# Laying out anew the pieces of a sorted second layer between the steps of a pair product

## The chip, the cores and the metric

The program runs on one core of one Trainium2 chip. The metric is the device time of one execution in microseconds (us); the median of the runs shown of the kernel before is 933.59 us (three runs, 932.44 to 934.21). Five engines work side by side, each through its own queue of instructions: PE multiplies matrices (its weight loads are listed apart as PEld), DVE does vector work, ACT does activations, POOL issues the indirect transfers here, and SP issues most of the others.

## The reference

Two images of 256 channels and 64 x 64 points (N = 4096 points) go through two layers. The first one is a 3 x 3 convolution to 64 channels, a normalisation and a PReLU; the similarity of all points, a sparse softmax over each row, and a weighted sum back onto the image. The change is in the second layer alone:

```python
g_x = jnp.einsum('oc,bcn->bno', g_w, xf) + g_b
a = jnp.einsum('c,bcn->bn', w_t, theta)
bsc = jnp.einsum('c,bcn->bn', w_p, phi)
f = jax.nn.relu(a[:, :, None] + bsc[:, None, :] + wf_b[0])
y = jnp.matmul(f / N, g_x)
...
z = W_y + xf
```

For each point n the layer sums g over the points m with a(n) + b(m) above zero, each with that sum as its weight. Written out, y(n) is a(n) times a sum of g(m) plus a sum of b(m) g(m), over the points whose b is above -a(n). If the points are sorted by b, both sums are prefix sums, and one row of a table of prefix sums is all that a point needs.

## The kernel before

The program does the second layer in two ways, one for each image, and lets them run beside each other.

**Image 1: pairs** (`by_pairs`, L662). After `attend(1)` (first layer, L442: 16 groups of four matmuls, and one DVE addition `x<-av,x` at L458 for each of eight column blocks) it forms `ga1` (`project`, L460: matmuls at L465 and a DVE addition at L472), spreads the row a over all partitions (`spread`, L476), and then runs the pair product: four quarters q of 1024 columns, 32 steps m each. A step makes f = relu(a + b) into one of four buffers (ACT at L676; in the last quarter every second one by DVE at L678) and multiplies it with g on PE (L680). After each quarter `finish` (L486) is called for two halves: ACT scales the sum (L690), PE multiplies with `wz` (L491), ACT writes `w` (L493, a tile with two buffers, tag "wb"), DVE adds it to `x` (L494) and SP stores the output (L495).

**Image 0: ranks** (`by_rank`, L497). It has no loop of its own: it hands pieces to the object `Beside`, which keeps them with a planned time. Each `beside.step(dt)` in the loops of image 1 moves a planned clock on and emits into the program the pieces that have fallen due: 3.6 a step in `attend`, 1.5 in the projection, 1.75 in the pair product. What is left over comes at the end, by `beside.rest()`. The pieces, in their order:

- `start`: spreads the row b into `bb` (S4) and takes `junk` (S5).
- `rank(t)`, 32 times: DVE counts for 128 points how many lie above them (L525, L528, L531, two small operations at L535 and L536), and POOL scatters those rows of g and b to their rank in the DRAM table `sg` (L537).
- `sorted_in`: reads the sorted rows back as two half tables `tab` (L548; S4 and S6, where S6 is the slot of `ga0`), and spreads the row a into `ab` (S5, after `junk`), by a PE transpose (L479), an ACT copy and two transfers.
- `products(0)`, `products(1)`: b times g (L562, L563). `sums`: 31 additions down the table, a row of 257 numbers each (L572).
- `before`: one PE product for the sums of the partitions before (`po`, L576), two DVE additions of it to the tables (L579) and two transfers to the DRAM table `tb` (L582).
- `segments`: two DVE operations make `oh` (L590, L591; S3) out of `ab`. `places(i)`, four times: 8 PE products `pk` (L599) and four DVE operations give the row of the table for 1024 points.
- `fetch(t)`, 32 times: POOL gathers 128 rows of `tb` into `r` (L614; S3, after `oh`; 16 places for 32 fetches). `taken(i)`, eight times: DVE at L625, PE transposes at L628, ACT at L630, and `finish`.

The tags S0 to S6 are slots of one buffer each: a tile waits until the tile before it in its slot is no longer read. The order of the program is not the order on the engines. When the program is built, a scheduling pass orders the instructions of each engine and adds the waits[...]. In the trace the small fill of `cnt` (L512, in `start`) runs 1.18 us after the span begins, though it stands in the program behind the whole first layer.

Of the kernel before, what the change touches and what calls it, by code (L numbers as in the profile page):

```python
# [8 lines left out]
F32 = mybir.dt.float32  # L9
# [10 lines left out]
P = 128  # L20
HW = 64
N = HW * HW
CB = 512
NCB = N // CB
NT = N // P
# [7 lines left out]
UN = 2 * CB  # L33
# [4 lines left out]
CS = 2 * CI + 1  # L38
TW = N // P
TH = TW // 2  # L40
# [45 lines left out]
def sparse_path(ctx: ExitStack, tc, a, out, rows_i):  # L86
# [7 lines left out]
    room = ctx.enter_context(tc.tile_pool(name="room", bufs=1))  # L94
# [388 lines left out]
        nc.sync.dma_start(out=rd.rearrange("o (t p) -> (o t) p", p=P), in_=row[0:nt])  # L483
        nc.sync.dma_start(out=dst[:, ds(t0 * P, nt * P)], in_=rd.to_broadcast((P, nt * P)))

    def finish(b, yT, cols):  # L486

        ov = out[b].rearrange("(k p) n -> p k n", p=P)
        for ct in range(CT):
            pz = ps_av.tile([P, CB], F32, name=f"pz_{b}_{ct}_{cols.start}", tag="av")  # L490
            nc.tensor.matmul(pz, lhsT=wz_sb[:, ts(ct, P)], rhs=yT, start=True, stop=True)  # L491
            w = work.tile([P, CB], F32, name=f"w_{b}_{ct}_{cols.start}", tag="wb")
            nc.scalar.activation(w, pz, AF.Identity, bias=b1[:, ct : ct + 1], scale=s1[:, ct : ct + 1])  # L493
            nc.vector.tensor_add(xs[b][:, ct, cols], w, xs[b][:, ct, cols])  # L494
            nc.sync.dma_start(out=ov[:, ct, cols], in_=xs[b][:, ct, cols])  # L495

    def by_rank(b, ga, beside):  # L497

# [4 lines left out]
        d = {}  # L503
# [40 lines left out]
        def sorted_in():  # L544
            sv = d["sg"].rearrange("(p t) c -> p t c", p=P)
            d["tab"] = [room.tile([P, TH, CS], F32, name=f"tab_{b}_{h}", tag=f"S{4 + 2 * h}") for h in range(2)]
            for h in range(2):
                nc.sync.dma_start(out=d["tab"][h][:, :, 0 : CI + 1], in_=sv[:, ts(h, TH)])  # L548
            nxt = small.tile([P, 1], F32, name=f"nxt_{b}", tag="nxt")
            nc.vector.memset(nxt, -3.0e38)  # L550
            nc.sync.dma_start(out=nxt[0 : P - 1], in_=sv[1:P, 0, CI : CI + 1])
            d["nxt"] = nxt
            d["ab"] = room.tile([P, N], F32, name=f"ab_{b}", tag="S5")
            spread(b, ga, CI + 1, d["ab"], 0, NT)

        def products(h):
            tab = d["tab"][h]
            if h == 0:
                d["kr"] = small.tile([P, TW + 2], F32, name=f"kr_{b}", tag="kr")
                nc.vector.memset(d["kr"][:, TW : TW + 1], 1.0)  # L560
                nc.vector.tensor_scalar_mul(d["kr"][:, TW + 1 : TW + 2], lane, float(TW))
            nc.vector.tensor_copy(d["kr"][:, ts(h, TH)], tab[:, :, CI])  # L562
            nc.vector.tensor_mul(  # L563
                tab[:, :, CI + 1 : CS], tab[:, :, 0:CI], tab[:, :, CI : CI + 1].to_broadcast([P, TH, CI])
            )
# [4 lines left out]
        def sums(t0, t1):  # L570
            for t in range(max(1, t0), t1):
                nc.vector.tensor_add(at(t), at(t), at(t - 1))  # L572
# [10 lines left out]

        def segments():

            oh = room.tile([P, N], F32, name=f"oh_{b}", tag="S3")
            lim = small.tile([P, 2], F32, name=f"lims_{b}", tag="lims")
            nc.vector.tensor_scalar_mul(lim[:, 0:1], d["kr"][:, 0:1], -1.0)
            nc.vector.tensor_scalar_mul(lim[:, 1:2], d["nxt"], -1.0)
            nc.vector.tensor_scalar(oh, d["ab"], lim[:, 0:1], None, ALU.is_gt)  # L590
            nc.vector.scalar_tensor_tensor(oh, d["ab"], lim[:, 1:2], oh, ALU.is_le, ALU.mult)  # L591
            d["oh"] = oh
            d["k"] = small.tile([P, NT], U32, name=f"k_{b}", tag="k")
# [16 lines left out]

        def fetch(t):
            if t == 0:
                d["r"] = room.tile([P, TH, CS], F32, name=f"r_{b}", tag="S3")
            nc.gpsimd.indirect_dma_start(  # L614
                out=d["r"][:, t % TH],
                out_offset=None,
                in_=d["tb"],
                in_offset=bass.IndirectOffsetOnAxis(ap=d["k"][:, t : t + 1], axis=0),
            )
# [17 lines left out]

        beside.add(0.0, start)
        beside.add(1.0, lambda: nc.vector.tensor_copy(acol, ga[:, :, CI + 1]))
        for t in range(NT):  # L640
            beside.add(11.0 + 5.6 * t, lambda t=t: rank(t))
        t1 = 11.0 + 5.6 * NT
        beside.add(t1, sorted_in)
        t1 += 10.0
        beside.add(t1, lambda: products(0))
        beside.add(t1 + 2.5, lambda: products(1))
        beside.add(t1 + 5.0, lambda: sums(0, TH))
        beside.add(t1 + 12.0, lambda: sums(TH, TW))
        beside.add(t1 + 19.0, before)
        beside.add(t1 + 28.0, segments)  # L650
        for i in range(4):
            beside.add(t1 + 35.0 + 2.0 * i, lambda i=i: places(i))
        t1 += 43.0
        for t in range(TH):
            beside.add(t1, lambda t=t: fetch(t))
        for i in range(8):
            beside.add(t1 + 8.0 + 5.5 * i, lambda i=i: taken(i))
            if i < 4:
                for t in range(4):
                    beside.add(t1 + 9.0 + 5.5 * i, lambda t=TH + 4 * i + t: fetch(t))  # L660

    def by_pairs(b, ga, beside):  # L662

        ab = room.tile([P, N], F32, name=f"ab_{b}", tag="S1")
        for i in range(NU):
            for m in range(8 * i, 8 * i + 8, 3):
                project(b, ga, m, min(m + 3, 8 * i + 8))
                beside.step(1.5)
            spread(b, ga, CI + 1, ab, 8 * i, 8)
        f = room.tile([P, 4, UN], F32, name=f"f_{b}", tag="S2")  # L670
        for q in range(NU):
            py = ps_sim.tile([P, UN], F32, name=f"py_{b}_{q}", tag="sim")
            for m in range(NT):
                bm = ga[:, m, CI : CI + 1]
                if q < NU - 1 or m % 2 == 0:
                    nc.scalar.activation(f[:, m % 4, :], ab[:, ts(q, UN)], AF.Relu, bias=bm)  # L676
                else:
                    nc.vector.tensor_scalar(f[:, m % 4, :], ab[:, ts(q, UN)], bm, 0.0, ALU.add, ALU.max)  # L678
                for h in range(2):
                    nc.tensor.matmul(  # L680
                        py[:, ts(h, CB)],
                        lhsT=ga[:, m, 0:CI],
                        rhs=f[:, m % 4, ts(h, CB)],
                        start=(m == 0),
                        stop=(m == NT - 1),
                    )
                beside.step(1.75)
            for h in range(2):
                yT = work.tile([P, CB], F32, name=f"yT_{b}_{q}_{h}", tag="wa")
                nc.scalar.activation(yT, py[:, ts(h, CB)], AF.Identity, scale=1.0 / N)  # L690
                finish(b, yT, ds(q * UN + h * CB, CB))

    got = [{}, {}]
    beside = Beside()
# [423 lines left out]
```

## Time and profile before

| | |
|---|---|
| median of the runs shown | 933.59 us |
| profiled execution, its own time | 934.23 us |
| its span, first to last instruction | 931.9 us |
| PE busy | 823.0 us (88%) |
| DVE busy | 551.5 us (59%) |
| ACT busy | 374.4 us (40%) |
| POOL busy | 112.7 us (12%) |
| `attend(1)` to the last addition | from 511 to 925 us of the span |

The span is 2.33 us shorter than the profiled execution's own time, and that execution took 0.64 us more than the median. Times in the trace count from the start of the span. A matmul of 512 columns on PE is two entries of some 0.43 us each from start to start, so that a step m of the pair product (four entries) takes 1.72 us. "Idle before" is the time in which an engine stood still before an instruction, and the arrow names what ended it. The chain of waits goes back from the last instruction to what released it.

### The profile page before, as it was taken

The numbers are of one execution on the slowest core, as the hardware profiler recorded it, in microseconds if no ns is written. First come the engines' busy times: TensorE is split into PE (matmuls) and PEld (weight loads), VectorE is DVE, ScalarE is ACT, GpSimd is POOL, SyncE is SP. The second block draws the span as 40 slices with busy tenths as digits, with TensorE's granted clock in tenths as the row PEclk, the third lists the DMA queues.
The fourth block names the chain that finished last, engine by engine and source line by source line (L and its number), as shares of the span: only waits on it lengthen the run. The fifth ranks groups of instructions, "written<-read, shape, count | busy, mean of one in ns | idle before, by whom it ended". The sixth has DMA issues, their size and how long they took to land.

```text
span 931.9 us, 8237 instructions
## 1 busy us (share of the span) xinstructions
PE 823.0 (88%) x3080; PEld 383.5 (41%) x3080; DVE 551.5 (59%) x794; ACT 374.4 (40%) x487; POOL 112.7 (12%) x95
## 2 busy tenths in 40 slices
PE   7999999999978889999898997269961999997996
PEld 3664444443323334444355443144420444453442
DVE  0105777774278676778257799999984005635432
ACT  0003676630066756650026000036622667633542
POOL 0000000008100000007200011111120000026500
PEclk9997999999999999999899998599985999998998
DMA  9202000011120000001100200021003005225411
GB/s 364 70 12 57 1 1 0 1 46 40 23 58 0 1 1 0 1 1 47 27 1 1 94 10 15 12 80 34 15 14 94 0 1 181 114 86 152 146 69 72
DMA packets 27412, 45.21 MB, mean 49 GB/s; under 512 B 11777, under 2 KB 16738, under 8 KB 26594
## 3 DMA queue, kind: packets, MB, share of 16 engines
q1 hardware_dynamic: 23730, 36.36, 11.3%
q0 software_dynamic: 3200, 7.64, 3.1%
q8 instruction: 26, 0.43, 0.2%
q10 hardware_dynamic: 432, 0.59, 0.2%
q14 instruction: 24, 0.20, 0.1%
HBM read 25.60 MB, written 16.88 MB: 46 GB/s over the span
## 4 chain that ended last, share of the span: by engine, by line
PE 62%; DVE 27%; ACT 4%; DMA 3%; issue 2%; POOL 1%; ACTq 0%; DVEq 0%; SPq 0%; POOLq 0%
PE sv L271 20%; PE py L680 16%; PE cv L221 13%; DVE junk L528 8%; DVE junk L525 8%; PE av L449 6%; DVE mq L418 3%; PE pz L491 2%; DVE top L289 2%; PE rw L271 1%; ACT z L417 1%; ACT z L433 1%; DVE z L435 1%; DVE junk L531 1%; POOL r L614 1%
## 5 line engine op out<-in xcount | busy, mean ns | idle before, releaser
L680 PE MATMUL py<-f,ga 128*128 128x512 f32 x512 | 230.6, 603 | 33.3 <-ACT f L676 27.4
L271 PE MATMUL sv<-e 64*128 64x512 f32 x1024 | 236.8, 605 | 13.3 <-DVE top L289 6.9
L289 DVE MAX8 top<-sv 128x8 f32<-128x1024 f32 x128 | 157.3, 1231 | 59.7 <-PE sv L271 59.5
L285 ACT ACTIVATE sv<-sv,nthr 128x1024 f32<-128x1024 f32 x128 | 139.3, 1088 | 76.5 <-ACT sv L285 52.0
L676 ACT ACTIVATE f<-ab,ga 128x1024 f32<-128x1024 f32 x112 | 127.8, 1147 | 82.2 <-PE py L680 80.0
L680 PEld LDWEIGHTS py<-f,ga 128*128 128x128 f32 x512 | 97.3, 193 | 150.4 <-issue 116.6
L271 PEld LDWEIGHTS sv<-e 64*128 64x128 f32 x1024 | 99.8, 189 | 140.7 <-ACT sv L285 62.0
L221 PE MATMUL cv<-x,w_sb 128*64 128x504 f32 (+3 forms) x576 | 128.3, 602 | 6.6 <-DMA w_sb<-in_conv_w 5.9
L449 PE MATMUL av<-z,xb 128*128 128x512 f32 x256 | 117.5, 618 | 6.6 <-DVE rk L535 5.1
L221 PEld LDWEIGHTS cv<-x,w_sb 128*64 128x64 f32 x576 | 60.7, 141 | 70.4 <-issue 41.9
L449 PEld LDWEIGHTS av<-z,xb 128*128 128x128 f32 x256 | 50.0, 198 | 70.5 <-issue 60.0
L528 DVE TENSOR_SCALAR_CACHE_REDUCE junk<-bb,ga 128x4096 f32<-128x4096 f32 (+31 forms) x32 | 77.4, 2417 | 0.0
L525 DVE TENSOR_SCALAR_CACHE_REDUCE junk<-bb,ga 128x128 f32<-128x128 f32 (+30 forms) x31 | 72.8, 2347 | 0.0
L494 DVE TENSOR_TENSOR x<-w,x 128x512 f32<-128x512 f32 x32 | 21.9, 689 | 67.1 <-ACT w L493 67.1
L537 POOL DMA_INDIRECT sg<-ga,rank x32 | 31.0, 970 | 218.9 <-DVE junk L531 121.4
L465 PE MATMUL g<-gw_sb,x 128*128 128x130 f32 x256 | 34.6, 288 | 23.9 <-DVE rk L535 19.8
L360 POOL TENSOR_TENSOR x<-x,mask 128x4096 f32<-128x4096 f32 x4 | 31.8, 7979 | 187.9 <-DMA mask<-kd 187.9
L418 DVE MAX8 mq<-z 128x8 f32<-128x1024 f32 x32 | 38.8, 1223 | 24.0 <-ACT z L417 23.9
L230 ACT ACTIVATE y<-cv,b,s 128x512 f32<-128x512 f32 x8 | 6.2, 777 | 114.4 <-PE cv L221 99.2
L614 POOL DMA_INDIRECT r<-tb,k x32 | 32.5, 1017 | 149.3 <-DVE above L603 132.5
L417 ACT COPY z<-rw 128x1024 f32<-128x1024 f32 x32 | 31.7, 1012 | 43.8 <-PE rw L271 43.8
L232 DVE TENSOR_SCALAR t<-y,v 128x512 f32<-128x512 f32 x8 | 3.9, 485 | 75.5 <-ACT y L230 75.5
(152 smaller groups left out, 494.8 us busy)
## 6 DMA issues: line engine op xcount, KB each, us to landing
x<-in_x SPq DMA_DIRECT2D x16, 512.0 KB
out<-x SPq DMA_DIRECT2D x32, 256.0 KB
tb<-tab SPq DMA_DIRECT2D x2, 2056.0 KB
tab<-sg SPq DMA_DIRECT2D x2, 1032.0 KB
e<-e SPq DMA_DIRECT2D x16, 128.0 KB
et<-es SPq DMA_DIRECT2D x16, 128.0 KB
mask<-kd SPq DMA_DIRECT2D x2, 1024.0 KB
bb<-rd SPq DMA_DIRECT2D x1, 2048.0 KB
```

The lines of the kernel that those rows point to most:

```text
L221: nc.tensor.matmul(p3[ts(h, CR), r0 - R * j : r1 - R * j, c0:c1], lhsT=w_sb[:, kc, 3 * dy + dx], rhs=x4[:, kc, r0 + dy - 1 : r1 + dy - 1, ...
L271: nc.tensor.matmul(ps[:, ts(h, CB)], lhsT=lhs(h), rhs=e[ts(h, CR), q], start=True, stop=True)
L285: nc.scalar.activation(ps, ps, AF.Relu, bias=nthr[:, i : i + 1], accum_out=over[:, i // 2, q : q + 1])
L289: nc.vector.max(m8[:, i // 2, ts(q, 8)], ps)
L417: nc.scalar.copy(zs[k][:, ts(q, UN)], ps)
L418: nc.vector.max(mq[:, k, ts(q, 8)], zs[k][:, ts(q, UN)])
L449: nc.tensor.matmul(ps[:, ct], lhsT=xb[:, k, ts(ct, P)], rhs=zs[k][:, ts(j, CB)], start=(k == 0), stop=(k == KB - 1),)
L525: nc.vector.tensor_scalar(junk[:, 0 : t * P], bb[:, 0 : t * P], bt, None, ALU.is_ge, ALU.add, accum_out=cnt[:, t, 0:1])
L528: nc.vector.tensor_scalar(junk[:, t * P : N], bb[:, t * P : N], bt, None, ALU.is_gt, ALU.add, accum_out=cnt[:, t, 1:2])
L614: nc.gpsimd.indirect_dma_start(out=d["r"][:, t % TH], out_offset=None, in_=d["tb"], in_offset=bass.IndirectOffsetOnAxis(ap=d["k"][:, t : t ...
L676: nc.scalar.activation(f[:, m % 4, :], ab[:, ts(q, UN)], AF.Relu, bias=bm)
L680: nc.tensor.matmul(py[:, ts(h, CB)], lhsT=ga[:, m, 0:CI], rhs=f[:, m % 4, ts(h, CB)], start=(m == 0), stop=(m == NT - 1),)
```

## The change

The pieces of image 0 get other planned times and in part another order; no arithmetic is changed.

- Ranks: seven at 11.0 + 6.6 t, none in the stretch of the projection ("beside g"), and the other 25 from 80 on at a distance of 6.4. Before, all 32 stood at 11.0 + 5.6 t.
- The spread of a leaves `sorted_in` and becomes a piece `spread_a` at 78. Its tile `ab` moves from S5 to S3, and `oh` and `r` move from S3 to S5.
- `sorted_in` falls at 243 (190.2 before), `products` at 255 and 258.5, `sums` in eight portions of four from 262 on at a distance of 2.6 (two portions before, at 205.2 and 212.2), `before` at 284 (219.2), `segments` at 286 (228.2), `places` from 295 on (235.2), the first fetches at 305 (243.2), `taken` from 314 on at a distance of 5.5 (251.2 before).
- `finish`, called from `by_pairs`, moves the planned clock by 0.9 after each of its outputs: 14.4 in all. The loops of image 1 together move it by 57.6 + 18.0 + 224.0 = 299.6 before and by 314.0 now.

```diff
-    def finish(b, yT, cols):
+    def finish(b, yT, cols, beside=None):
...
             nc.sync.dma_start(out=ov[:, ct, cols], in_=xs[b][:, ct, cols])
+            if beside is not None:
+                beside.step(0.9)
...
             d["nxt"] = nxt
-            d["ab"] = room.tile([P, N], F32, name=f"ab_{b}", tag="S5")
+
+        def spread_a():
+            d["ab"] = room.tile([P, N], F32, name=f"ab_{b}", tag="S3")
             spread(b, ga, CI + 1, d["ab"], 0, NT)
...
-            oh = room.tile([P, N], F32, name=f"oh_{b}", tag="S3")
+            oh = room.tile([P, N], F32, name=f"oh_{b}", tag="S5")
...
-                d["r"] = room.tile([P, TH, CS], F32, name=f"r_{b}", tag="S3")
+                d["r"] = room.tile([P, TH, CS], F32, name=f"r_{b}", tag="S5")
...
-        for t in range(NT):
-            beside.add(11.0 + 5.6 * t, lambda t=t: rank(t))
-        t1 = 11.0 + 5.6 * NT
+        t0, t1 = 11.0, 61.0
+        early = 7
+        for t in range(early):
+            beside.add(t0 + 6.6 * t, lambda t=t: rank(t))
+        t1 = 61.0 + 17.0
+        beside.add(t1, spread_a)
+        for t in range(early, NT):
+            beside.add(t1 + 2.0 + 6.4 * (t - early), lambda t=t: rank(t))
+        t1 += 2.0 + 6.4 * (NT - early) + 3.0
         beside.add(t1, sorted_in)
-        t1 += 10.0
+        t1 += 12.0
         beside.add(t1, lambda: products(0))
-        beside.add(t1 + 2.5, lambda: products(1))
-        beside.add(t1 + 5.0, lambda: sums(0, TH))
-        beside.add(t1 + 12.0, lambda: sums(TH, TW))
-        beside.add(t1 + 19.0, before)
-        beside.add(t1 + 28.0, segments)
+        beside.add(t1 + 3.5, lambda: products(1))
+        for i in range(8):
+            beside.add(t1 + 7.0 + 2.6 * i, lambda i=i: sums(4 * i, 4 * i + 4))
+        beside.add(t1 + 29.0, before)
+        t1 += 31.0
+        beside.add(t1, segments)
         for i in range(4):
-            beside.add(t1 + 35.0 + 2.0 * i, lambda i=i: places(i))
-        t1 += 43.0
+            beside.add(t1 + 9.0 + 2.0 * i, lambda i=i: places(i))
+        t1 += 19.0
         for t in range(TH):
             beside.add(t1, lambda t=t: fetch(t))
         for i in range(8):
-            beside.add(t1 + 8.0 + 5.5 * i, lambda i=i: taken(i))
+            beside.add(t1 + 9.0 + 5.5 * i, lambda i=i: taken(i))
             if i < 4:
                 for t in range(4):
-                    beside.add(t1 + 9.0 + 5.5 * i, lambda t=TH + 4 * i + t: fetch(t))
+                    beside.add(t1 + 10.0 + 5.5 * i, lambda t=TH + 4 * i + t: fetch(t))
...
-                finish(b, yT, ds(q * UN + h * CB, CB))
+                finish(b, yT, ds(q * UN + h * CB, CB), beside)
```

## The prediction, made before the changed kernel was run

> **What bounds the kernel now.** I read the page first, and then the answers of the trace from 511 us on, where the change lies: all waits, the DVE, PE and POOL queues in order of time, and busy time by stage.
>
> ```profile
> PE 823.0 (88%) x3080; PEld 383.5 (41%) x3080; DVE 551.5 (59%) x794; ACT 374.4 (40%) x487; POOL 112.7 (12%) x95
> ```
>
> PE carries the whole, but 88% is a mean. The list of waits (engine, line, what it waited for; us in all, times, longest) names where PE is not fed in this part:
>
> ```profile
> PE py L680 <- ACT f L676: 27.4, 1, 27.4
> ACT w L493 <- DVE x L494: 33.9, 3, 31.9
> PE g L465 <- DVE rk L535: 19.8, 1, 19.8
> DVE kr L562 <- DMA tab<-sg: 18.2, 2, 11.1
> PE py L680 <- DVE r L625: 5.0, 1, 5.0
> POOL r L614 <- DVE above L603: 132.5, 1, 132.5
> ```
>
> The largest, 27.4 us, lies from 690.59 to 718.00. Read from its end: PE waits for f, f stands in ACT's queue behind a `w` of the first finish (31.9), that one waits for a `w` buffer, which DVE's addition to x frees, and the addition comes late in DVE's queue. That queue, in order of time (start, length):
>
> ```profile
> 696.21 0.15 DVE L536 CAST rank<-rk 128x1 uint32<-128x1 f32 x1
> 707.51 0.17 DVE L562 COPY kr<-tab 128x16 f32<-128x16 f32 x1 [11.14 <-DMA tab<-sg]
> 707.60 2.29 DVE L563 TENSOR_TENSOR tab<-tab 128x2048 f32<-128x2048 f32 x1
> 709.80 0.15 DVE L588 TENSOR_SCALAR lims<-kr 128x1 f32<-128x1 f32 x1
> 709.86 0.15 DVE L589 TENSOR_SCALAR lims<-nxt 128x1 f32<-128x1 f32 x1
> 709.92 4.57 DVE L572 TENSOR_TENSOR tab<-tab 128x257 f32<-128x257 f32 x10
> 714.41 0.69 DVE L494 TENSOR_TENSOR x<-w,x 128x512 f32<-128x512 f32 x1
> ```
>
> Here is the observation on which everything below rests. The addition of the first finish (planned clock 131.6) stands behind the last rank (planned 184.6), the products (200.2), ten sums (205.2) and the two limits of `segments` (228.2). So a planned time didn't hold these pieces back: the pass that ordered DVE took them as soon as their inputs were there in its own reckoning. The ranks show the same:
>
> ```profile
> 587.80 1.24 DVE L458 TENSOR_TENSOR x<-av,x 128x1024 f32<-128x1024 f32 x1
> 589.00 1.68 DVE L525 TENSOR_SCALAR_CACHE_REDUCE junk<-bb,ga 128x1408 f32<-128x1408 f32 x1
> 593.79 1.82 DVE L525 TENSOR_SCALAR_CACHE_REDUCE junk<-bb,ga 128x1536 f32<-128x1536 f32 x1
> 598.52 1.24 DVE L458 TENSOR_TENSOR x<-av,x 128x1024 f32<-128x1024 f32 x1
> ```
>
> 1408 and 1536 columns are 11 and 12 blocks of 128: ranks 11 and 12 run before the last addition of `attend`. In the program, 57.6 planned units have passed at that addition, enough for ranks 0 to 8 only. PE is different: it has always work ready, and its queue keeps the planned places. `po` (219.2, that is 18 steps into the third quarter) runs at 803.64, 17 steps of 1.72 after its start at 774.5; `pk` and the transposes of `taken` fit as well.
>
> **What the Trainium skill says.** "TensorE: Matmul & The Clock Gate", section on the array as 16 x 32x32: the queues of ScalarE and VectorE are strictly first in, first out. The trace agrees: f waits 27.4 us behind a `w` that it doesn't need. "Perfetto Trace Analysis", Optimization Strategy: regimes with different bounds may gain by being interleaved. That is the plan of the change; here it needs the order on the queue to follow the plan. "DMA: Bandwidth & Descriptors", Issuing engines are not separate DMA queues: all transfers share 16 engines. Two half tables read together therefore share them; no wait of before shows this, since they are 73 us apart.
>
> **The change, part by part.**
>
> *Ranks apart, none beside g.* The ranks' inputs (`bb`, `ga0`) are there from the first one on. On DVE, nothing is nearer in the program and ready when they run, as shown; moving them back in the program leaves them the filling of the same idle time. I take 0 us. The 171 us from 524.9 to 696.2 stay, with the 19.8 us wait of g and the start of the long stall at 690.59. Bounds: 0, and the first rival.
>
> *Spread of a early.* One PE transpose (0.3), one ACT copy (0.25), two transfers on SP. Before, `bb`'s of the same size was issued at 516.22 and used by 524.89, so it lasts at most 8.7 us; S3 is free after `attend`, and the pair product needs only its first columns of its own `ab` then. Covered by the ranks' 171 us: 0; without that cover at most 8.7. What it does do: `ga0`, the slot of the second half table, is free after the last rank. Before, the transpose stood in PE's queue at 774.35, and the second half was read at 775.04. Now it is read right behind the first, at some 702.
>
> *What fills the end of the long stall.* DVE gets ready at about 707.5 not only the first half, but also the second product (0.17 + 2.29) and, since a is spread, the two operations of `segments`, 2.35 (L590) and 4.48 (L591). In the trace of before, those two slipped in among sums of higher place at 791.0 and 793.6, so they do fill gaps. If none comes ahead of the two additions that release ACT, the cost is 0. If the product and L590 do: the second half lands at about 712 (estimate: 707.5 plus the transfer again, 5.96 us from issue to landing with some 1.5 of it before data), then 2.5 + 2.35 + 0.4 for a sum, and the two additions 1.4: 718.6 against 716.04, +2.6. With L591 and another sum +7.5. I take +5, PE restarts at 723.0; ends 0 and 9.
>
> *Sums in portions, steps in finish.* The same 31 sums of 0.43; DVE is idle from 719 to 770, so all are done there: 0. The 0.9 steps only move the planned clock.
>
> *Later places on PE.* Here the plan counts. Clock 284 (`po`) is 17 steps into the last quarter (which starts at 254.4), the four `places` come after 24, 25, 26 and 27 steps, and `taken` at 314, behind everything of the pair product. From the restart: before, 718.00 to 834.39 is 116.4; without `po` (0.4) and the places (4 x 1.71 = 6.9) 109.1. The finish at 834.39 to 838.20: 3.8. Then 27 x 1.715 = 46.3, with `po` 0.4 and places 6.9. The two additions L579, 8.8 us on DVE (2 x 4.43), now stand where DVE makes every second f. A buffer gives it some 5 us of lead, one f comes before: 2 us of PE wait (0 to 5). Sum 168.5. The last `pk` ends at 723.0 + 168.5 = 891.5.
>
> *The tail that now stands alone.* Fetches wait until `oh` is read for the last time, since `r` takes its slot:
>
> ```profile
> 830.03 1.87 PE L599 MATMUL pk<-kr,oh 128*128 128x34 f32 x16
> 832.68 0.98 POOL L614 DMA_INDIRECT r<-tb,k  x1 [132.55 <-DVE above L603]
> 833.96 1.43 POOL L614 DMA_INDIRECT r<-tb,k  x1 [0.30 <-issue]
> ```
>
> 0.8 us after the last `pk` POOL starts. Twenty fetches in a row took 26.0 us (832.68 to 858.65), 1.30 each; the last of 32 starts 31 x 1.30 = 40.3 later: 932.6. Before, this ran under the last quarter. Now only four steps and a finish (some 11 us) are left to cover it. `tb` isn't late: the additions end at about 877, and the last transfer of before (issued 813.1) was in by 832.7. Data come 2.8 us after a fetch starts (832.68, 835.50): 935.4. DVE, transposes, ACT, and the last finish: 907.65 to 913.22 is 5.6 less 1.7 of pair product, plus 0.5 before: 4.4, so 939.8. From there to the end 7.1 (924.76 to 931.9). Span 946.9. With 2.3 around it 949.2, less 0.6 that the profiled execution stood above the median: 948.6. I say **948**: +15 from 934, of which 5 are the stall and some 10 the tail.
>
> **The rivals.**
> 1. *The plan is obeyed* (faster). If DVE keeps the planned places, 25 ranks go under the pair product, where DVE is idle, and the stalls of 27.4, 19.8 and 5.1 (`attend` behind ranks) vanish. PE: `attend` from 519.1 takes 55, g 18.5, the pairs 4 x 58.7 = 235, `po` and places 7, waits 4: 839. The last `pk` is 12 before that, 827, and the chain above adds 55: 882 + 2, **885**. Deciding point: the ranks' order between the L458. The four lines above speak against it.
> 2. *The additions pass ahead of the sorted half* (faster): if two reads at once delay the first half in the pass's reckoning by more than the 7.2 us of DVE work that stood between landing and addition, ACT is released at 696 and not 714. 948 - 5 - 18 = **925**.
> 3. *`po` and `places` slip forward on PE*: their inputs are ready some 90 us earlier. If PE has gaps in the pass's reckoning, they and `taken` fill them, and the tail is gone. The PE work is the same; +5, less 5.9 of PE waits of the last quarter: **933**, no change. Against it: before, `pk` didn't slip, though `oh` was ready 21 us earlier.
> 4. *Worse tail*: f's of DVE queued behind additions and `taken`s that wait for fetches, +10 and more: **960**.
>
> **How the numbers follow.** The forecast has 0.60, its own range is 941 to 956; rivals 1 to 4 have 0.07, 0.08, 0.13, 0.12. From 930 to 958 lies the forecast, nearly all of the third rival and half of the fourth; outside stay the first two and the upper end of the fourth, 0.2. No change means within 0.2% (931.7 to 935.5), about what this measurement can tell. Faster: 0.07 + 0.08 + 0.04 of the third = 0.19; same 0.05; slower 0.76.
>
> **What would show it.** Right: ranks 11 and 12 still before the last L458; one stall of PE of 27 to 36 us near 691; the second `tab` read at about 702; all L628 behind the last L680; POOL's fetches from about 892 to 933. Wrong: ranks found after 700 (rival 1), L494 ahead of L562 (2), `pk` well before 870 (3).

## The result and the profile after

The changed kernel takes 958.24 us (median of four runs, 955.27 to 962.36) where the kernel before, run beside it, takes 933.69 us: a ratio of 1.0268, interval 1.0223 to 1.0313. So it is slower by 24.6 us. The forecast was 948 us.

The profiled execution was the longest of the four, 962.36 us with a span of 960.5 us. In its trace PE stands still for 7.1 us at a place where the second profile of the same kernel, taken in the fifth experiment (954.77 us, span 952.9 us), shows 3.1 us (below). Both profiles are used here. In the changed kernel the lines behind the edits are a few further on: L680 is L691, f's L676 and L678 are L687 and L689, `kr` is L566, `segments` L592 to L595, `po` L580, `pk` L603, the fetch L618, the sum over fetched rows L629 and the transposes L632.

The first part of the page after, busy time by engine (share of the span, number of instructions):

```profile
PE 833.4 (87%) x3080; PEld 387.4 (40%) x3080; DVE 550.7 (57%) x794; ACT 374.5 (39%) x487; POOL 111.2 (12%) x95
```

The same number of instructions on PE and DVE as before. PE's 10.4 us more of busy time are not more work: in the tail, where `taken` runs alone, its `pz` are busy 22.9 us (15.7 before) and its transposes 7.0 us (4.8), because single entries last longer there, as shown below.

The list of waits of the kernel after, from 519 us on (engine, line, what it waited for; us in all, times, longest):

```profile
POOL r L618 <- PE pk L603: 186.4, 1, 186.4
...
ACT w L493 <- DVE x L494: 44.7, 3, 32.5
...
PE py L691 <- ACT f L687: 27.7, 1, 27.7
...
PE g L465 <- DVE rk L537: 19.8, 1, 19.8
...
DVE kr L566 <- DMA tab<-sg: 11.4, 1, 11.4
...
PE py L632 <- ACT w L493: 11.2, 2, 10.6
```

The two large waits of PE are where they were, 27.7 us (27.4 before) and 19.8 us (19.8): the new layout removed neither. What grew is POOL's wait for the last `pk` (132.5 before, 186.4 now). What is new is the last line: the first transposes of `taken` stand 10.6 us behind a `w` of `finish`. Before, the two halves of the table were waited for apart (18.2 us in two waits); now there is one wait of 11.4 us, because both are read together. From its issue to its first use the first half takes 6.40 us (701.09 to 707.49), against 5.99 us when it was read alone (701.52 to 707.51).

DVE's queue of the kernel after in order of time (start, length), at `attend`'s last two additions and at the end of the long stall:

```profile
587.52 1.22 DVE L458 TENSOR_TENSOR x<-av,x 128x1024 f32<-128x1024 f32 x1
...
588.72 1.67 DVE L527 TENSOR_SCALAR_CACHE_REDUCE junk<-bb,ga 128x1408 f32<-128x1408 f32 x1
...
593.52 1.80 DVE L527 TENSOR_SCALAR_CACHE_REDUCE junk<-bb,ga 128x1536 f32<-128x1536 f32 x1
...
598.25 1.22 DVE L458 TENSOR_TENSOR x<-av,x 128x1024 f32<-128x1024 f32 x1
...
707.49 0.17 DVE L566 COPY kr<-tab 128x16 f32<-128x16 f32 x1 [11.42 <-DMA tab<-sg]
707.58 2.28 DVE L567 TENSOR_TENSOR tab<-tab 128x2048 f32<-128x2048 f32 x1
...
709.90 0.43 DVE L576 TENSOR_TENSOR tab<-tab 128x257 f32<-128x257 f32 x1
710.24 2.35 DVE L594 TENSOR_SCALAR oh<-ab,lims 128x4096 f32<-128x4096 f32 x1
...
712.59 2.29 DVE L567 TENSOR_TENSOR tab<-tab 128x2048 f32<-128x2048 f32 x1
714.79 1.28 DVE L494 TENSOR_TENSOR x<-w,x 128x512 f32<-128x512 f32 x2
...
716.79 4.48 DVE L595 SCALAR_TENSOR_TENSOR oh<-ab,lims,oh 128x4096 f32<-128x4096 f32 x1
```

Ranks 11 and 12 (1408 and 1536 columns) still run before the last L458, although their planned times were moved back. Ahead of the two additions L494, which release ACT, there now stand one sum, L594 and the second product, where ten sums stood before. The work differs, the length does not: the first of these additions starts at 714.79 (before 714.41), and PE goes on at 718.10 (before 718.00).

The tail of the kernel after, from its timeline (start, length, engine, line):

```profile
883.97 1.87 PE L603 MATMUL pk<-kr,oh 128*128 128x34 f32 x16
...
886.11 0.98 POOL L618 DMA_INDIRECT r<-tb,k  x1 [186.41 <-PE pk L603]
...
895.19 3.98 PE L491 MATMUL pz<-yT,wz_sb 128*128 128x512 f32 x8 [0.69 <-issue]
...
905.12 0.94 POOL L618 DMA_INDIRECT r<-tb,k  x1 [0.30 <-issue]
...
907.89 0.35 DVE L629 SCALAR_TENSOR_TENSOR r<-r,acol 128x128 f32<-128x128 f32 x1 [0.88 <-DMA r<-tb,k]
908.16 1.29 DVE L494 TENSOR_TENSOR x<-w,x 128x512 f32<-128x512 f32 x2
908.94 1.45 ACT L493 ACTIVATE w<-pz,b,s 128x512 f32<-128x512 f32 x2 [10.95 <-DVE x L494]
...
909.77 1.12 PE L632 MATMUL py<-ident,r 128*128 128x128 f32 x4 [10.60 <-ACT w L493]
910.52 1.41 POOL L618 DMA_INDIRECT r<-tb,k  x1 [4.46 <-PE py L632]
...
929.75 3.78 PE L491 MATMUL pz<-yTs,wz_sb 128*128 128x512 f32 x4 [7.10 <-issue]
929.85 0.94 POOL L618 DMA_INDIRECT r<-tb,k  x1 [0.31 <-issue]
...
952.67 0.69 DVE L494 TENSOR_TENSOR x<-w,x 128x512 f32<-128x512 f32 x1
```

This is to be read from the middle. The pair product's last finish starts its `pz` at 895.19. Its third `w` needs a buffer (w has two), which an addition L494 on DVE gives back. Ahead of that addition stand 16 sums L629 in DVE's queue, each behind the landing of one fetch. The last of them is at 907.89, so the addition comes at 908.16, `w` at 908.94 and the first transposes of `taken` at 909.77, though the rows they need had been there since some 893. (The transposes wait for `w` because they write into the two PSUM buffers that `pz` uses too; such a buffer is free when `w` has been read from it.) POOL, which had filled all 16 places of `r`, waits 4.46 us for these transposes before it may write over the first of them. The last fetch starts at 929.85, and the last addition ends at 953.36, 23.5 us later. Before, `taken` ran among the steps of the last quarter: its last `pz` (909.81) came ahead of the last products (911.52), so none of its chain stood behind them.

### The profile page after: what moved, and what is told of

Same layout as the page of the kernel before. It is cut to its first block, busy times and chain, and to the rows that moved or that the text cites. A ratio compares the mean times of both kernels' runs of the same rounds, so it can differ in the third digit from the quotient of the medians.

```text
span 960.5 us, 8265 instructions
## 1 busy us (share of the span) xinstructions
PE 833.4 (87%) x3080; PEld 387.4 (40%) x3080; DVE 550.7 (57%) x794; ACT 374.5 (39%) x487; POOL 111.2 (12%) x95
## 4 chain that ended last, share of the span: by engine, by line
PE 60%; DVE 27%; ACT 4%; issue 4%; DMA 3%; POOL 1%; ACTq 0%; DVEq 0%; SPq 0%; POOLq 0%
PE sv L271 20%; PE py L691 15%; PE cv L221 13%; DVE junk L530 8%; DVE junk L527 7%; PE av L449 6%; PE pz L491 3%; DVE mq L418 3%; DVE top L289 2%; PE rw L271 1%; ACT z L417 1%; POOL r L618 1%; ACT z L433 1%; DVE z L435 1%; DVE junk L533 1%
## 5 line engine op out<-in xcount | busy, mean ns | idle before, releaser
L691 PE MATMUL py<-f,ga 128*128 128x512 f32 x512 | 227.0, 603 | 27.7 <-ACT f L687 27.7
L687 ACT ACTIVATE f<-ab,ga 128x1024 f32<-128x1024 f32 x112 | 127.9, 1147 | 99.5 <-PE py L691 98.6
L691 PEld LDWEIGHTS py<-f,ga 128*128 128x128 f32 x512 | 98.4, 194 | 148.9 <-issue 119.8
L689 DVE TENSOR_SCALAR f<-ab,ga 128x1024 f32<-128x1024 f32 x16 | 12.0, 753 | 78.3 <-PE py L691 78.3
L465 PE MATMUL g<-gw_sb,x 128*128 128x130 f32 x256 | 34.6, 289 | 23.9 <-DVE rk L537 19.8
L618 POOL DMA_INDIRECT r<-tb,k x32 | 31.1, 971 | 200.0 <-PE pk L603 186.4
L494 DVE TENSOR_TENSOR x<-w,x 128x512 f32<-128x512 f32 x32 | 21.7, 690 | 55.5 <-ACT w L493 55.5
L493 ACT ACTIVATE w<-pz,b,s 128x512 f32<-128x512 f32 x32 | 24.2, 776 | 64.8 <-DVE x L494 44.7
```

Source lines behind the costliest of these rows:

```text
L465: nc.tensor.matmul(ps[:, m - m0], lhsT=xs[b][:, kc, ts(m, P)], rhs=gw_sb[:, kc, :], start=(kc == 0), stop=(kc == CT - 1),)
L618: nc.gpsimd.indirect_dma_start(out=d["r"][:, t % TH], out_offset=None, in_=d["tb"], in_offset=bass.IndirectOffsetOnAxis(ap=d["k"][:, t : t ...
L691: nc.tensor.matmul(py[:, ts(h, CB)], lhsT=ga[:, m, 0:CI], rhs=f[:, m % 4, ts(h, CB)], start=(m == 0), stop=(m == NT - 1),)
```

## The experiments

All ratios are against the kernel before, run in turn with the experiment on the same chip.

**1. Only the late places.** The kernel before, with everything from `before()` on planned as late as in the change, and nothing else:

```diff
-        beside.add(t1 + 19.0, before)
-        beside.add(t1 + 28.0, segments)
+        late = 284.0 - 14.4
+        beside.add(late, before)
+        beside.add(late + 2.0, segments)
...
-            beside.add(t1 + 35.0 + 2.0 * i, lambda i=i: places(i))
-        t1 += 43.0
+            beside.add(late + 11.0 + 2.0 * i, lambda i=i: places(i))
+        t1 = late + 21.0
...
-            beside.add(t1 + 8.0 + 5.5 * i, lambda i=i: taken(i))
+            beside.add(t1 + 9.0 + 5.5 * i, lambda i=i: taken(i))
```

> The kernel before with one thing of the change: the product po, the places, the fetches and the taken pieces at the late planned times, counted from the end of the plan as in the change (30 units ahead of it for po, 19 for the places, none for the first taken); ranks, spread of a, slots, sums and finish as before. Theory (the whole loss is the tail of image 0 that stands alone after the pair product): 950 to 962, all transposes of taken behind the last pair product. Rival (the loss comes from the spread, the slots, the portions or the ranks): 934, within 3 us of the kernel before.

Measured: 954.61 us (951.55 to 955.93), ratio 1.0217 (1.0185 to 1.025). POOL's fetches go from 884.8 to 929.5 there, against 886.11 to 929.85 in the kernel after. The late places alone give the loss of the change within the two intervals.

**2. All but the late places.** The ranks apart and none beside g, a spread early in S3, `oh` and `r` in S5, the sums in eight portions; `before`, `segments`, `places`, the fetches and `taken` at the planned times of the kernel before, and no steps in `finish`. The later ranks stand 5.5 apart, not 6.4:

```diff
-        for t in range(NT):
-            beside.add(11.0 + 5.6 * t, lambda t=t: rank(t))
+        for t in range(7):
+            beside.add(11.0 + 6.6 * t, lambda t=t: rank(t))
+        for t in range(7, NT):
+            beside.add(80.0 + 5.5 * (t - 7), lambda t=t: rank(t))
+        beside.add(78.0, spread_a)
...
-        beside.add(t1 + 5.0, lambda: sums(0, TH))
-        beside.add(t1 + 12.0, lambda: sums(TH, TW))
+        for i in range(8):
+            beside.add(214.0 + 0.5 * i, lambda i=i: sums(4 * i, 4 * i + 4))
```

> The rest of the change alone: ranks apart and none beside g (5.5 apart behind the gap, so that they end before po's old time), spread of a at 78, the three slots exchanged, sums in eight portions; po, places, fetches and taken at the times of before, and the planned clock not moved by finish. Theory: 932 to 936, the stall of PE near 691 still 27 to 28 us, rank 13 still ahead of the last addition of attend. Rival 1 of the prediction (the plan orders the ranks): 890 to 910. Rival that these parts cost something: above 940.

Measured: 934.16 us, ratio 1.0002 (0.9989 to 1.0014). These parts are worth nothing that can be measured; with the first experiment, the late place is the whole of the loss, as far as the intervals can tell. The 0.9 of `finish` is in neither kernel by itself.

**3. The last finish with buffers of its own.** The kernel after, where the finish of the last half of the last quarter takes `w` from two further buffers:

```diff
-            w = work.tile([P, CB], F32, name=f"w_{b}_{ct}_{cols.start}", tag="wb")
+            w = (
+                work.tile([P, CB], F32, name=f"w_{b}_{ct}_{cols.start}", tag="wp", bufs=2)
+                if own
+                else work.tile([P, CB], F32, name=f"w_{b}_{ct}_{cols.start}", tag="wb")
+            )
...
-                finish(b, yT, ds(q * UN + h * CB, CB), beside)
+                finish(b, yT, ds(q * UN + h * CB, CB), beside, own=q == NU - 1 and h == 1)
```

> The changed kernel, where the second half's finish of the last quarter has two buffers of its own for w, so that the four w there don't wait for DVE's additions behind sixteen operations of taken. Theory (PE's 10.6 us wait before the first transpose of taken comes from that w): the transposes begin near 899 and not 910, POOL's wait of 4.5 us after 16 fetches goes, 948 to 953. Rival (the tail is held by its own chain of one taken after the other, whenever it begins): within 3 us of the changed kernel, 955 to 960.

Measured: 953.15 us (950.7 to 953.16), ratio 1.0198 (1.0171 to 1.0226). That is at the upper edge of what was expected, 948 to 953. PE's queue in the tail of this kernel (its transposes are L636, its `w` L497), and one line of ACT's:

```profile
900.01 0.66 PE L636 MATMUL py<-ident,r 128*128 128x128 f32 x4
901.41 1.98 PE L491 MATMUL pz<-yTs,wz_sb 128*128 128x512 f32 x4 [0.75 <-ACT yTs L638]
909.76 1.45 ACT L497 ACTIVATE w<-pz,b,s 128x512 f32<-128x512 f32 x2 [8.40 <-DVE x L498]
910.59 1.12 PE L636 MATMUL py<-ident,r 128*128 128x128 f32 x4 [7.20 <-ACT w L497]
```

The first `taken` is no longer held up, and the fetches go on without their pause. But the second one meets the same wait one step later, 7.2 us: the first one's `w` (909.76) needs the two shared buffers, which the finish of the first half still holds, and its additions stand behind the 16 sums on DVE as before. The wait was moved by one `taken`, not removed; the gain is some 3 to 5 us (953.15 against 956.36 and 958.24).

**4. Four buffers for w in the kernel before.** The same edit in the kernel before, for h = 1 of every quarter (`own=h == 1`). It asks what the stall near 691 is worth:

> The kernel before, where the second half's finish in every quarter has two buffers of its own for w (four in all instead of two). Theory (the 27 us stall is ACT's w waiting for a buffer, with the f's queued behind it, while the DVE order is unchanged): the stall goes, PE runs on at 691, and the end comes 24 to 28 us earlier, 906 to 911. Rival (PE would then wait for something else that DVE is late with, such as the additions for the PSUM or the table): less than 8 us of gain, above 926.

Measured: 905.37 us (904.11 to 907.09), ratio 0.9702 (0.9676 to 0.9727), faster than both kernels and 0.6 us below what was expected. PE's queue at the place of the long stall, in the timeline of this kernel (the pair product is L684 here):

```profile
684.63 41.79 PE L684 MATMUL py<-f,ga 128*128 128x512 f32 x97
```

and DVE's at the same time:

```profile
715.70 0.69 DVE L498 TENSOR_TENSOR x<-w,x 128x512 f32<-128x512 f32 x1
```

DVE's addition comes as late as ever, at 715.70, but no one waits for it: PE runs 97 entries without a pause. So the stall was a matter of two buffers: without touching the order on DVE, two more take it away.

**5. The kernel after, profiled again.**

> The changed kernel as it is, profiled a second time. Theory (the tail's own chain of eight takens sets the end): about 957 us, 955 to 962, ratio 1.025; the last quarter's finish again waits some 10 us for a w buffer, POOL again some 4.5 us ahead of its 17th fetch, and from the start of the last fetch to the last addition of the finish lie about 16 to 24 us, not the 7.2 of the prediction. Rival (the hole of 7.1 us near 922 in the first profile belongs to that one execution and is most of the excess): the hole is gone and the stretch from the last fetch to the last addition shrinks to some 16 us, with a time near 955; if the hole belongs to the kernel, it stands again at the same place.

Measured: 956.36 us (954.36 to 959.86), ratio 1.0248 (1.0214 to 1.0283). PE's queue of this execution in the tail:

```profile
909.10 1.11 PE L632 MATMUL py<-ident,r 128*128 128x128 f32 x4 [10.69 <-ACT w L493]
...
921.27 0.66 PE L632 MATMUL py<-ident,r 128*128 128x128 f32 x4
925.07 3.78 PE L491 MATMUL pz<-yTs,wz_sb 128*128 128x512 f32 x4 [3.14 <-ACT yTs L634]
928.64 1.06 PE L632 MATMUL py<-ident,r 128*128 128x128 f32 x4
930.39 3.78 PE L491 MATMUL pz<-yTs,wz_sb 128*128 128x512 f32 x4 [0.69 <-ACT yTs L634]
933.96 0.88 PE L632 MATMUL py<-ident,r 128*128 128x128 f32 x4
935.53 1.98 PE L491 MATMUL pz<-yTs,wz_sb 128*128 128x512 f32 x4 [0.69 <-ACT yTs L634]
```

The wait of 10.6 us is there again (10.69), and so is POOL's, 4.53 us. The hole of 7.1 us ahead of `pz` at 929.75 of the first profile, which the trace puts down to nothing it shows, is down to 3.14 us, which are a wait for `yTs`. So it does not come in every execution; whether the unprofiled ones (955.27 to 960.31 us in the two groups of runs) had it is not known. From the start of the last fetch (930.15) to the end of the last addition (945.77) are 15.6 us here, against 23.5.

**6 and 7. The block earlier.** The kernel after with one number changed, the distance of the later ranks' planned times, which carries everything behind them along:

```diff
+        step = 6.4 - 20.0 / 25
...
-            beside.add(t1 + 2.0 + 6.4 * (t - early), lambda t=t: rank(t))
-        t1 += 2.0 + 6.4 * (NT - early) + 3.0
+            beside.add(t1 + 2.0 + step * (t - early), lambda t=t: rank(t))
+        t1 += 2.0 + step * (NT - early) + 3.0
```

(40.0 in place of 20.0 in the seventh.)

> After with one number changed: the step between the later ranks' planned times 5.6 units in place of 6.4, so that the whole block from the sorted table's read on is planned 20 units earlier; PE's order then has po after 11 products of the last quarter in place of after its end, and four of the eight takens inside the quarter. Theory (only the place of the block costs): between the two kernels, about 941 us, 936 to 948, ratio 1.003 to 1.015, with a wait of POOL on pk some 20 us shorter. Rival (something else of the new layout costs, such as the ranks' spacing or the portions): 955 us or more.

> As the run before with a step of 4.8 units: the block planned 40 units earlier, po inside the third quarter, seven of the eight takens begun before the last product. Theory: about the time of the kernel before, 934 us, 930 to 938, ratio 0.996 to 1.004, since before has the same arrangement. Rival (something else costs): 945 us or more. A second rival: with the block even earlier than this nothing more is gained, since the pair products themselves then bound the end.

Measured, beside the two kernels (times of the fetches from each profile; those of the kernel after from its second one):

| | planned time of `before()` | time, us | ratio (interval) | fetches from | to |
|---|---|---|---|---|---|
| after | 284 | 956.36 | 1.0248 (1.0214 to 1.0283) | 885.4 | 930.2 |
| 20 earlier | 264 | 946.91 | 1.0134 (1.0112 to 1.0156) | 866.2 | 918.8 |
| 40 earlier | 244 | 937.87 | 1.0038 (1.002 to 1.0056) | 845.7 | 894.9 |

The time falls by 9.4 and 9.0 us for 20 units each, in line with the place as the only cause, and both fall inside what was expected. The seventh is still 0.4% over the kernel before; its `po` runs at 821.37, 17.7 us later than in that kernel (803.64).

**8. The rest of the change where the stall is gone.** The kernel of the second experiment with the four buffers of the fourth:

> The second experiment's kernel (all of the change but the late planned times) with the fourth experiment's buffers (the finishes of h = 1 take w from two buffers of their own, in every quarter). Theory (the parts of the change other than the place are worth nothing even where the stall near 691 is gone): 905 us, 902 to 908, as the kernel before with those buffers. Rival (the nearer ranks and portions were hidden only by that stall, and now show): a gain or a loss of more than 4 us, below 901 or above 909.

Measured: 904.9 us (903.58 to 905.38), ratio 0.9688 (0.9667 to 0.9709). The fourth has 0.9702 (0.9676 to 0.9727). Even without the stall these parts of the change give nothing.

**9. Four buffers in the kernel after.**

> The changed kernel with own w buffers for the finishes of h = 1 in every quarter, as in the fourth experiment. Theory (two separate costs: the stall near 691 of some 28 us, and the tail behind the late block): the stall and the last finish's wait for w both go, PE runs out of pair products some 28 us earlier, near 865; po then follows 33 products of the last quarter at about 848, the last pk ends near 874, POOL's 32 fetches without their wait last till 914, and some 15 us of takens and 7 us of end follow: about 937 us, 930 to 944, which is still some 32 us over the kernel before with the same buffers (905.4). Rival (the late block costs only because the stall pushes po back as well): below 920 us.

Measured: 922.57 us (920.59 to 923.73), ratio 0.9885 (0.986 to 0.991). That is neither the 930 to 944 of the theory nor below 920. The number of the theory was worked out wrongly: 33 products, two to a step, stand ahead of `po` in this quarter, some 28 us, and the theory put `po` at 848, some 20 us too late. It runs at 827.87, which is 30.9 us ahead of its 858.76 in the kernel after, so what the stall had cost comes back in full at this point, and the rest follows. So this run's own bound did not decide; the sum over the four kernels is of more use:

| | w in two buffers | w in four | difference |
|---|---|---|---|
| block at its old place | 933.9 | 905.4 | -28.6 |
| block late | 956.4 | 922.6 | -33.8 |
| difference | +22.4 | +17.2 | |

The late block costs 17 us with four buffers too, so it is a cost of its own. The 5.2 us by which the corner deviates are of the size that the third experiment took out of the tail, and this kernel contains the third's edit; that this is their cause was not tested by itself.

**10. Dead work in the tail.** In the tail many entries of `pz` last twice as long (3.78 us for four against 1.98). To see whether PE's holes are the cause, each `taken` got eight products more, of 128 columns, into a tile that no one reads: added work, with no part in the output.

```diff
                 nc.tensor.transpose(py[:, t % 4], r[:, 0:CI], ident)
+                dead = 1 if t % 4 < 3 else 5
+                for _ in range(dead):
+                    nc.tensor.matmul(dm[:, 0:P], lhsT=r[:, 0:CI], rhs=ident, start=True, stop=True)
```

> The changed kernel with eight dead products of 128 columns on PE beside each taken's four transposes (work added, its result read by no one), so that PE has fewer holes in the tail. Theory (in the tail PE runs at half its clock because it is idle half of the time, and that lengthens the takens' chain): the entries of pz for the takens last 2.0 us a pair at every taken, none 3.8; the time is 950 to 957 us, since the dead products stand in the chain themselves. Rival (the lower clock isn't set by the holes): three or more takens still show 3.8 us, and the time is 958 to 966 us.

Measured: 960.51 us (959.87 to 962.19), ratio 1.0296 (1.0273 to 1.0319). PE's queue of this kernel at the takens that were slow in the fifth:

```profile
928.52 1.88 PE L491 MATMUL pz<-yTs,wz_sb 128*128 128x512 f32 x4
...
935.88 1.98 PE L491 MATMUL pz<-yTs,wz_sb 128*128 128x512 f32 x4 [1.72 <-ACT yTs L640]
...
940.16 1.88 PE L491 MATMUL pz<-yTs,wz_sb 128*128 128x512 f32 x4
```

Busy time by stretches of the same kernel (us of each engine with the number of instructions; then PE's granted clock, the DMA engines' share, GB/s):

```profile
931.00:953.00 22.00, 17.11 (x98) 11.59 (x98) 8.77 (x17) 10.06 (x14) 2.25 (x3) 1.00 0.44 154
```

and of the kernel after, first profile:

```profile
931.00:953.00 22.00, 17.66 (x37) 7.09 (x36) 7.40 (x15) 9.93 (x14) 0.00 (x0) 0.67 0.30 108
```

From the second `taken` on no `pz` lasts longer than 2 us, and the clock is 1.00 where it was 0.67 (0.81 in the second profile). So the lower clock goes when PE's holes are filled; that part of the theory held. The Trainium skill describes it in "TensorE: Matmul & The Clock Gate", section "HAM oscillation": there a loop's repeated waits for transfers put the array back to half its clock each time. In the trace of the kernel after the granted clock is 0.50 from 905 to 914 us, from within the wait of 10.6 us on, and again from 926 to 944 us; a group of four `pz` entries takes 3.78 us there and 1.98 at full clock. But the time did not fall into the 950 to 957; it lies in the rival's 958 to 966. The dead products stand in the same chain: at full clock the last two `pz` groups start 4.17 us apart with them (944.33 and 948.50) and 3.34 apart without (938.90 and 942.24 in the fifth's profile). Nothing is gained by warming PE this way.

**11. Eight places for w in the tail.** The kernel after, where the finishes of the last quarter and of the eight `taken` write `w` into eight places of slot S3, which is free by then; the order of PE's and DVE's queues is unchanged:

```diff
-            w = work.tile([P, CB], F32, name=f"w_{b}_{ct}_{cols.start}", tag="wb")
+            if own:
+                if ws[0] is None:
+                    ws[0] = room.tile([P, 8, CB], F32, name=f"ws_{b}", tag="S3")
+                w = ws[0][:, ws[1] % 8]
+                ws[1] += 1
+            else:
+                w = work.tile([P, CB], F32, name=f"w_{b}_{ct}_{cols.start}", tag="wb")
...
-            finish(b, yT, ds(i * CB, CB))
+            finish(b, yT, ds(i * CB, CB), own=True)
...
-                finish(b, yT, ds(q * UN + h * CB, CB), beside)
+                finish(b, yT, ds(q * UN + h * CB, CB), beside, own=q == NU - 1)
```

> The changed kernel, where the finishes of the last quarter and of the eight takens write w into eight places of the slot S3, which is free there, in place of the two buffers of the pool; the order of the instructions on PE and DVE is that of the changed kernel. Theory (what the prediction left out of the tail is that w's two buffers tie PE and ACT to DVE, where 16 sums of fetched rows stand ahead of the last quarter's additions): the transposes of the first taken start right behind the last quarter's finish, near 898.5, POOL's wait ahead of the 17th fetch goes, the last fetch starts near 925 and the last addition ends 7 to 9 us after it, so that span is about 940 and the time 942 us, 939 to 945. Rival (the takens' own chain on PE and ACT, with PE at half its clock, is what is long): last fetch as before near 930, or 14 us or more from the last fetch to the last addition; 949 us or more.

Measured: 946.71 us (945.78 to 948.31), ratio 1.0141 (1.0124 to 1.0158). The tail of this kernel in its timeline (transposes L640, fetches L626, additions L502):

```profile
895.91 3.98 PE L493 MATMUL pz<-yT,wz_sb 128*128 128x512 f32 x8 [0.69 <-ACT yT L709]
...
899.91 0.66 PE L640 MATMUL py<-ident,r 128*128 128x128 f32 x4
...
907.09 0.95 POOL L626 DMA_INDIRECT r<-tb,k  x1 [0.30 <-PE py L640]
...
927.56 0.98 POOL L626 DMA_INDIRECT r<-tb,k  x1 [0.30 <-PE py L640]
...
933.33 3.57 PE L493 MATMUL pz<-yTs,wz_sb 128*128 128x512 f32 x4 [0.75 <-ACT yTs L642]
...
937.74 0.69 DVE L502 TENSOR_TENSOR x<-ws,x 128x512 f32<-128x512 f32 x1 [0.35 <-ACT ws L501]
```

The first transposes come right behind the finish (899.91 in place of 909.77), POOL's pause is gone, and from the last fetch to the end of the last addition 10.9 us are left (927.56 to 938.43) in place of 15.6. (Eight places for 20 `w` are not quite enough: one `w` still waits 1.58 us for an addition, at 909.65.) The time lies 1.7 us above the range expected and 2.3 us below the rival's. What is missing is seen in the lines: the last fetch at 927.56 and not 925, since POOL's pace was slower for a few fetches, and the last `taken` at half clock (3.57 in place of 1.98). Of the 22.4 us that the late block costs, the two buffers of `w` in the tail make about 10 (956.36 against 946.71). The other 13 us no run takes apart; what is left standing there are the fetches and the last `taken` themselves, which run on for 38.5 us after PE's part of the last finish (899.89 to 938.43), with nothing beside them. More PSUM buffers in place of more `w` buffers were not tried.

## Why the forecast was off

The forecast had the direction right: slower, because the tail stands alone behind the pair product. Its size was too small, 948 against 958.24, and the step that failed is "The tail that now stands alone": it put the stretch from the first fetch to the last addition at 40.3 + 7.2 us, and that stretch took 60.4 us in the second profile and 67.2 us in the first. The terms of the sum, with what the two executions of the changed kernel show:

| | forecast | first profile | second |
|---|---|---|---|
| PE goes on after the long stall | 723.0 | 718.10 | 717.37 |
| from there to the end of the last `pk` | 168.5 | 167.7 | 167.7 |
| from there to the start of the first fetch | 0.8 | 0.3 | 0.3 |
| first fetch to last fetch, start to start | 40.3 | 43.7 | 44.8 |
| start of the last fetch to the end of the last addition | 7.2 | 23.5 | 15.6 |
| from there to the end of the span | 7.1 | 7.1 | 7.1 |
| span | 946.9 | 960.5 | 952.9 |

"Ranks apart, none beside g", at 0: right. Ranks 11 and 12 stand where they stood, the waits of 19.8 us and 27 us stay, and the second experiment, with the ranks 5.5 apart, gives a ratio of 1.0002. The observation on which it rested, that planned times hold nothing back on DVE, held.

"Spread of a early" and "Sums in portions, steps in finish", at 0: the spread and the portions right by the same run, and by the eighth, where the stall that might have hidden them is gone. The steps in `finish` have no run of their own. The second half table was read right behind the first, as forecast (both issued between 701.1 and 701.8).

"What fills the end of the long stall", at +5: the pieces came as described, the second product, L594 and one sum ahead of the additions, and the long L595 behind the first two. But the sum put all of them one after another behind the second half's landing at 712. In the trace the sum and L594 (709.90 to 712.59) ran while that half was still awaited, and only the product and the additions came after. It measured +0.1 (-0.6 in the second profile). By luck this error hides 5 us of the other: without it the forecast would have been 943.

"Later places on PE", 168.5 us: right, 167.7 in both. The wait of 2 us in it measured 0.40. On PE the plan held for `po` and for the last two `places`.

"The tail that now stands alone" had the mechanism right and its size wrong. It took the pace of the fetches from a row of before and then only one `taken` behind the last fetch, 7.2 us. That assumes that the other seven keep up with the fetches. They did not: the first began 10.6 us late behind a `w` buffer, POOL lost 4.5 us on the place that it frees, and then four `taken`s were left to do, one after another on PE and ACT, partly at half clock. In the second profile the two terms of the table that concern it (44.8 and 15.6 against 40.3 and 7.2) make +12.9 us; the earlier restart and the shorter way to the last `pk` make -6.4, the start of the first fetch -0.5; 946.9 + 6.0 = 952.9, which is the span. The eleventh experiment shows the cause of most of it: with `w` in places of its own the same order of queues is 9.7 us shorter, and the two terms are 40.7 and 10.9 us, so that 4.1 of the 12.9 us stay. In the first profile 7.1 us more are the hole.

Of the rivals, the first (plan obeyed) did not come; its sum, 882 + 2, makes 884 and not 885. The third (pieces slip forward on PE) came only in part: two of the four `places` ran earlier than planned, at 866.05 and 868.32, but the last two stayed, and only the last one counts. The second did not come: two reads at once delayed the first half by 0.4 us, and its product (707.58) still ran ahead of the additions. The fourth, 960 us, comes nearest in time, and its idea is half right: something on DVE stands behind operations that wait for fetches. It is not the f's, which were all done before the first fetched rows came, but the additions of the last finish, and through two `w` buffers ACT and PE with them. The mechanism was in view before: the same `w`, the same addition and the same two buffers make the long stall of 27.4 us that the prediction reads from its end. It was not carried over to the new tail. Two more lines of the kernel before point to it, one of the list of waits and one of ACT's queue:

```profile
POOL r L614 <- PE py L628: 8.3, 3, 3.7
840.86 0.78 ACT L493 ACTIVATE w<-pz,b,s 128x512 f32<-128x512 f32 x1 [3.68 <-DVE r L625]
```

POOL waited 8.3 us for transposes there too, behind the row of 20 fetches whose pace was taken; and a `w` already waited 3.68 us for an addition (840.08) behind a sum of fetched rows.

What stays open: the hole of 7.1 us in one of the two profiles. The trace names no releaser on PE, and ACT's `yTs` ahead of it waits 5.00 us for a release whose source the profile doesn't show. The ninth kernel's 7.24 us ahead of its second `taken` is another thing: it stands where the third has 7.20 us, its `w` (878.08) right behind DVE's additions (877.30). Open too is why the clock stays at 0.50 for 20 us of the first profile's tail and for 10 in the second's, where most waits between groups are 0.69 us.

## What to carry to other kernels

When a piece loses its cover, do not price only the last link behind its last transfer: write down all links of the chain that now stands alone, and for each the buffers that tie it to an in-order queue, above all one whose head waits for transfers. A stall whose end is a buffer can be cured at the buffer: two more tiles of `w` gave 28.6 us, while moving 25 ranks about in the plan gave nothing. In this kernel moving a piece in the plan moved it on PE, which has other work ready nearly all the time (`po` and the last `places`), and did not move the ranks on DVE, which is idle for long stretches. So look in the trace at what the order on the queue is before pricing a change of the plan.

## What the runs showed that was not expected

The four buffers of `w` take 3% off the kernel before (0.9702, interval 0.9676 to 0.9727), the best of all runs together with the eighth. PE runs at half its clock in parts of the tail: a group of four `pz` entries lasts 3.78 us instead of 1.98, and a few dead products restore the clock without any gain in time. And most fetches of 128 rows through an index go out every 1.25 us (0.95 of POOL and 0.30 to the next) while nothing holds POOL; the prediction's 1.30 is the mean of a row in which a few took up to 1.43 us.
